# Three more batches of layer 1's keys and values made inside layer 0's quantized feed-forward, in a two-layer perceiver kernel

## The chip, the cores and the metric

The kernel runs on one core of one Trainium2 chip. The metric is the device time of one execution in microseconds (us); the median of three runs is compared. The core has four compute engines that each work through their own queue in order: PE (matrix multiply), DVE and ACT (elementwise work and reductions) and POOL (small work), and a fifth, SP, which here only issues DMA transfers.

## The reference, cut to what matters

Two layers work on `x` of 64 batches by 32 tokens by 256 features. Each has a cross-attention to a context of 257 rows a batch, a self-attention and a feed-forward, each on a layer norm of `x` and added to it. The change touches the feed-forward of layer 0 and the cross-attention of layer 1:

```python
def _L0_ffn_ref(x, w_gate, w_up, w_down):
    x = act_qdq(x)                                  # round to 16 bits, one scale for all of x
    up = act_qdq(x @ lpbq_dequant(w_up).T)
    gate = act_qdq(x @ lpbq_dequant(w_gate).T)
    sig = fixed_qdq_u16(jax.nn.sigmoid(gate))
    gate = act_qdq(gate * sig)
    o = act_qdq(gate * up)
    return o @ lpbq_dequant(w_down).T

def _L1_xattn_ref(x1, x2, Wq, bq, Wk, bk, Wv, bv, Wo, bo):
    q = x1 @ Wq.T + bq
    k = x2 @ Wk.T + bk                              # x2 is the context: 64 x 257 x 256
    v = x2 @ Wv.T + bv
    ...
    scores = jnp.einsum('bhnd,bhmd->bhnm', q, k) * scale
    attn = jax.nn.softmax(scores, axis=-1)
    o = jnp.einsum('bhnm,bhmd->bhnd', attn, v)
    ...
    return o @ Wo.T + bo

x = x + _L0_ffn_ref(_layernorm(x, axis=-1), ...)
x = x + _L1_xattn_ref(_layernorm(x, axis=-1), ctx_1024, ...)
```

`act_qdq` takes the largest absolute value of its whole input before it can round any of it, so the feed-forward is a row of stages with a global maximum between them. The keys and values of layer 1 depend on the context alone, not on `x`, so they can be made at any time.

## The kernel before, in words

**Keys and values made ahead.** Thirteen of layer 1's 64 batches (`AHEAD`, L566) have their keys and values made before layer 1 and kept in DRAM: four (`EARLY`) at the end of layer 0's self-attention, nine (`LATER`: 19, 23, ... 51) in its feed-forward. For one batch of `LATER`, `ahead_products` (L620) loads the batch's context, `ct`, over SP (two buffers), and issues 16 matmuls on PE: eight for the keys (`keys_of`, L591) and eight for the values (`values_of`, L602). Their results take three PSUM banks with the tag `mm`, of which there are six in this stage. `ahead_kept` is `ahead_keys` and `ahead_values`: on ACT two biased copies of the keys (L597, into `kb`, two buffers) and one copy of the values (L636, into `vb`, three buffers), and on SP two stores to DRAM, `dk` (L632) and `dv` (L638). The document calls an `ahead_kept` a keep.

**The stage between the up and the down projection.** The gate `g` and the up projection `u` each lie in 12 chunks of 128 x 1024. When the scale of the gate product is known, a loop over the chunks runs (L1147 on): `round_h(c + 1)` rounds a chunk of `g` and `round_up(n_up)` a chunk of `u`, both on ACT (L1108, L1105). `product(c)` multiplies the two on DVE and takes the maximum of the result (L1112 and L360); it needs `round_h(c)` and `round_up(c)` done. At some values of `c` the loop calls `keep_next` (L1139), which keeps the next batch and then issues the products of the batch after the next; so two batches' products are in flight, in the six banks. Two keeps and the first products stand before the loop (L1115 on, in the order written there), one keep behind it and two in the down projection. Behind the loop `scale_of` makes the scale of the output (`so`, `ro`), and `round_out` and `unbias` round it in blocks of 256 tokens, alternately on ACT and DVE. The down projection (L1185) takes a block at a time: 24 matmuls each.

**Layer 1's cross-attention** is a loop over the 64 batches, `f` (L1664 on), with the self-attention of the same layer interleaved in it, in steps that repeat every eight `f`. Step `f` issues `scores(f)` on PE, `weigh(f - 2)` on PE, `maxima(f)` on DVE (L1309), then the keys and values of batch `f + 1` (PE L591, L602; ACT L597; DVE L618), the exponentials `exps(f)` on ACT (L1316), `weights(f - 1)` on DVE (L1326, L1328) and the transposes `turn(f - 1)` on PE (L1347), whose results ACT and DVE copy. `scores(f + 1)` writes the same four PSUM banks that `exps(f)` reads. Where batch `f + 1` was made ahead, the step is "short" and in another order: its keys and values are loaded from DRAM (`kb` at step `f - 1`, L1700, `vb` in the step, L1716), no context is prefetched, and `weights(f - 1)` comes before `maxima(f)`, `turn(f - 1)` directly after it.

The order of the instructions on PE, DVE, ACT and POOL is the order of the program text there (`manual_schedule`). SP's order is left to the framework. Line numbers are those of the profile.

## Time and profile before

| | us |
|---|---|
| median of 3 runs (lowest, highest) | 1313.03 (1312.58, 1313.61) |
| the profiled execution, its own time | 1315.9 |
| its span, first to last instruction | 1314.0 |
| PE busy | 1221.6 (93%) |
| DVE busy | 908.0 (69%) |
| ACT busy | 722.1 (55%) |
| POOL busy | 157.9 (12%) |
| mean granted PE clock, of full | 0.977 |

A profile's page gives one execution. A group of instructions is named by its line, its engine, its operation and its tiles, as `out<-in`; `PEld` is the loading of weights into PE, which overlaps the matmuls. The chain of waits is followed back from the last instruction, at each step to what released it. In the timeline a row has the start, the time from there to the end of the last instruction of the row, the engine, the line, the operation and the number of instructions merged; in brackets stands the engine's idle time before it and what ended it. In a table of windows each row is a stretch of the span with its length, the busy time of each engine in it (and its number of instructions), and then the granted PE clock as a share of full speed, the share of time that the DMA engines were busy and what they moved in GB/s. All times are counted from the start of the span.

### The profile page before, as it was taken

The page shows a single profiled execution, that of the slowest core. Times are in us where ns is not written, and L with a number is a line of the kernel's source. Part 1 is how long each engine was busy: PE and PEld are TensorE (multiplying, and loading weights), DVE is VectorE, ACT ScalarE, POOL GpSimd, SP SyncE. Part 2 cuts the span into 40 slices and gives each one's busy share as a digit, 9 for nine tenths or more (in the row PEclk, how much of TensorE's full clock was granted, in tenths as well). Part 3 has the DMA queues.
Part 4 walks back from the last instruction along what each step waited for, and adds up shares of the span by engine and source line. Part 5 has one row for each costly group of instructions (what it writes and reads, how often), then busy time and mean ns, then how long its engine had stood idle before and what let it go on. Part 6 is the DMA issues. An engine that isn't in the chain of part 4 may idle for free.

```text
span 1314.0 us, 28426 instructions
## 1 busy us (share of the span) xinstructions
PE 1221.6 (93%) x11696; PEld 949.5 (72%) x11696; DVE 908.0 (69%) x1783; ACT 722.1 (55%) x1519; POOL 157.9 (12%) x418
## 2 busy tenths in 40 slices
PE   7899999999779998999999999998779999999998
PEld 5687877643568776767777777776557888888887
DVE  6878888768983688768788887868666363453633
ACT  4887887428792355657676766665525221221311
POOL 3111221000001022221212121211100000000000
PEclk9999999999999999989999999999769999999999
DMA  9200000630240442211111111100025000000000
GB/s 280 28 26 2 27 1 13 202 128 0 75 134 9 131 126 70 58 39 53 54 46 47 46 46 54 47 22 18 1 71 201 21 17 0 16 1 1 16 0 18
DMA packets 65430, 70.50 MB, mean 54 GB/s; under 512 B 21328, under 2 KB 52880, under 8 KB 65296
## 3 DMA queue, kind: packets, MB, share of 16 engines
q1 hardware_dynamic: 64864, 68.40, 17.7%
q8 instruction: 94, 1.54, 0.5%
q14 instruction: 40, 0.33, 0.1%
q10 hardware_dynamic: 432, 0.24, 0.1%
HBM read 59.63 MB, written 8.99 MB: 52 GB/s over the span
## 4 chain that ended last, share of the span: by engine, by line
PE 49%; DVE 15%; ACT 9%; issue 2%; DMA 2%; SPq 0%; POOL 0%; DVEq 0%; ACTq 0%
PE mm L1852 21%; PE mm L591 4%; PE mm L602 3%; PE mm L1347 3%; PE o L1185 3%; DVE nm L1309 2%; PE mm L397 2%; PE o L1919 2%; PE s L1298 2%; DVE mx L360 2%; DVE pe L1328 2%; ACT pe L1316 2%; ACT pb L312 2%; PE mm L348 1%; PE o L1367 1%
## 5 line engine op out<-in xcount | busy, mean ns | idle before, releaser
L1852 PE MATMUL mm<-hl,f_h 128*128 128x512 f32 x1024 | 232.9, 389 | 1.3 <-ACT sl L1897 1.3
L1852 PEld LDWEIGHTS mm<-hl,f_h 128*128 128x128 f32 x1024 | 192.1, 188 | 41.4 <-issue 1.5
L591 PE MATMUL mm<-ct,x_wk 128*128 128x257 f32 x512 | 132.5, 402 | 15.8 <-ACT kb L597 13.7
L1316 ACT ACTIVATE pe<-s,nm 128x257 f32<-128x257 f32 x256 | 118.5, 483 | 47.3 <-DVE nm L1309 20.8
L1910 ACT ACTIVATE g<-mm,cols 128x512 f32<-128x512 f32 x64 | 44.1, 689 | 163.9 <-PE mm L1852 163.5
L1858 DVE CAST hl<-g 128x512 fp32r<-128x512 f32 x64 | 27.3, 427 | 147.5 <-ACT g L1910 147.5
L591 PEld LDWEIGHTS mm<-ct,x_wk 128*128 128x128 f32 x512 | 95.6, 196 | 37.7 <-ACT kb L597 15.7
L602 PE MATMUL mm<-x_wv,ct 128*128 128x256 f32 x512 | 121.3, 380 | 0.3 <-ACT vb L636 0.3
L602 PEld LDWEIGHTS mm<-x_wv,ct 128*128 128x128 f32 x512 | 97.2, 190 | 14.4 <-ACT vb L636 0.7
L312 ACT ACTIVATE pb<-pt,masks 128x1024 f32<-128x1024 f32 x90 | 96.8, 1141 | 14.9 <-DVE pt L303 14.4
L597 ACT ACTIVATE kb<-mm,cols 128x257 f32<-128x257 f32 x128 | 57.8, 476 | 55.2 <-PE mm L591 51.3
L1309 DVE TENSOR_REDUCE nm<-s 128x4 f32<-128x1028 f32 x64 | 78.2, 1221 | 11.5 <-PE s L1298 11.5
L1336 POOL TENSOR_TENSOR px<-pe,rec 32x4 f32<-32x4 f32 x256 | 51.0, 199 | 264.7 <-DVE rec L1326 219.5
L1328 DVE TENSOR_SCALAR pe<-pe,rec 128x256 f32<-128x256 f32 x256 | 78.8, 370 | 5.7 <-DVE rec L1326 0.5
L1347 PE MATMUL mm<-ident,pe 128*128 128x128 f32 x512 | 75.9, 282 | 7.0 <-DVE pe L1328 4.5
L1347 PEld LDWEIGHTS mm<-ident,pe 128*128 128x128 f32 x512 | 59.2, 141 | 23.6 <-issue 5.9
L415 POOL TENSOR_TENSOR x<-x,rows 128x512 f32<-128x512 f32 x32 | 46.7, 1458 | 135.8 <-DVE xn L369 129.9
L1316 ACT ACTIVATION_READ_ACCUMULATOR pe<-s,nm 128x1 f32 x256 | 54.8, 214 | 0.0
L1298 PE MATMUL s<-kb,qb 32*64 32x257 f32 x1024 | 45.4, 409 | 8.9 <-ACT pe L1316 5.4
L1352 DVE COPY pT<-mm 128x512 f32<-128x512 f32 x64 | 44.0, 688 | 11.1 <-PE mm L1347 10.5
L1367 PEld LDWEIGHTS o<-pT,vb 128*32 128x32 f32 x2048 | 32.6, 112 | 25.1 <-issue 20.3
L618 DVE COPY vb<-mm 128x512 f32<-128x512 f32 x51 | 34.9, 685 | 21.2 <-PE mm L602 18.7
(238 smaller groups left out, 2363.4 us busy)
## 6 DMA issues: line engine op xcount, KB each, us to landing
ct<-in_ctxT_dram SPq DMA_DIRECT2D x64, 257.0 KB, 2.8
raw<-in_f_h_dram SPq DMA_DIRECT2D x20, 512.0 KB, 4.3
wck<-in_f_h_dram SPq DMA_DIRECT2D x12, 512.0 KB, 3.5
raw<-in_f_w_dram SPq DMA_DIRECT2D x8, 512.0 KB, 3.7
dk<-kb SPq DMA_DIRECT2D x13, 257.0 KB, 3.5
kb<-dk SPq DMA_DIRECT2D x13, 257.0 KB, 2.6
dv<-vb SPq DMA_DIRECT2D x13, 256.0 KB, 3.4
vb<-dv SPq DMA_DIRECT2D x13, 256.0 KB, 2.6
```

The costliest lines, as they stand in the source:

```text
L312: nc.scalar.activation(dst, src, AF.Copy, scale=scale)
L415: nc.gpsimd.tensor_tensor(xs, xs, bc(row(name), 1, 2), ALU.add)
L591: nc.tensor.matmul(pm, lhsT=x1_wk[:, k, m * P : (m + 1) * P], rhs=ct[:, k, :], start=(k == 0), stop=(k == 1),)
L597: nc.scalar.activation(kb[:, m, :], pm, AF.Identity, bias=col("x1_bk", m))
L602: nc.tensor.matmul(pm[:, c * D : (c + 1) * D], lhsT=ct[:, k, c * P : (c + 1) * P], rhs=x1_wv[:, k, :], start=(k == 0), stop=(k == 1),)
L1298: nc.tensor.matmul(sc[64 * m : 64 * m + 64, r, :S], lhsT=qb[rs, m, b % 4].rearrange("p h l -> p (h l)"), rhs=kb[rs, m, :], start=True, sto ...
L1309: nc.vector.tensor_reduce(w["nm"], w["sc"][:, :, :S], AX.X, ALU.max, negate=True)
L1316: nc.scalar.activation(w["pe"][:, r, :], w["sc"][:, r, :S], AF.Exp, bias=w["nm"][:, r : r + 1], accum_out=w["sums"][:, r : r + 1],)
L1328: nc.vector.tensor_scalar(pe[:, r, :SK], pe[:, r, :SK], rec[:, r : r + 1], None, ALU.mult)
L1336: nc.gpsimd.tensor_tensor(x4[j * L : (j + 1) * L, q // 2, :, q % 2], pe[of, :, SK], rec[of], ALU.mult)
L1347: nc.tensor.transpose(pt[:, r * P : (r + 1) * P], pe[:, r, c * P : (c + 1) * P], ident)
L1852: nc.tensor.matmul(pm, lhsT=w[:, k, c0 : c0 + P], rhs=hl[k][:, part, :], start=(k == 0 and part == 0), stop=(k == kt - 1 and part == 1),)
```

## The change

Batches 11, 25 and 41 are put in front of `LATER`, so 16 batches are made ahead instead of 13, and 48 are made in layer 1. In the loop between the up and the down projection `keep_next` is called at seven values of `c` instead of four, and `round_up` is called in every turn as long as chunks are left, also in those with a keep (so its last call is at `c` = 7 instead of 10). Behind the loop the program text is the same: one keep there and one in each of the first two blocks of the down projection. In layer 1, `f` = 10, 24 and 40 take the short order.

```diff
-    LATER, EARLY = tuple(range(19, 52, 4)), (15, 55, 59, 63)
+    LATER, EARLY = (11, 25, 41) + tuple(range(19, 52, 4)), (15, 55, 59, 63)
     AHEAD = LATER + EARLY
...
                 if c + 1 < NC:
                     round_h(c + 1)
                 product(c)
-                if c in (1, 4, 7, 11):
+                if c in (1, 3, 5, 7, 8, 10, 11):
                     keep_next()
-                elif n_up < NC:
+                if n_up < NC:
                     round_up(n_up)
                     n_up += 1
```

## The prediction, made before the changed kernel ran

> **What bounds the kernel now.** I read the page's chain of waits first: it runs mostly over PE (49%), then DVE (15%) and ACT (9%). Then I cut the span into the stages that the change touches: the rounding loop with the kept batches up to the first down-projection matmul (354.2 to 388.0), the down projection (388.0 to 437.2) and layer 1's cross-attention (437.2 to 911.7).

> ```profile
> core 0: us, PE busy (x) PEld busy (x) DVE busy (x) ACT busy (x) POOL busy (x), PEclk, DMA share, GB/s
> 354.20:388.00 33.80, 21.79 (x83) 17.39 (x83) 31.37 (x33) 30.99 (x37) 0.35 (x1) 0.90 0.36 117
> 388.00:437.20 49.20, 48.46 (x225) 41.63 (x224) 14.82 (x24) 14.86 (x18) 5.88 (x8) 1.00 0.17 50
> 437.20:911.72 474.52, 453.75 (x5678) 346.54 (x5682) 380.60 (x892) 312.66 (x923) 92.76 (x310) 0.99 0.20 57
> ```

> In the first stage PE idles for 12.0 us while DVE and ACT are full; in the other two PE is busy 98% and 96%. So products moved from the third stage into the first look free. Where the 12 us lie decides it, so next I read PE's timeline of the first stage.

> ```profile
> 366.14 2.00 PE L591 MATMUL mm<-ct,x_wk 128*128 128x257 f32 x8 [1.63 <-ACT kb L597]
> 367.98 1.89 PE L602 MATMUL mm<-x_wv,ct 128*128 128x256 f32 x8
> 373.00 3.46 PE L591 MATMUL mm<-ct,x_wk 128*128 128x257 f32 x8 [3.13 <-ACT kb L597]
> 376.30 1.89 PE L602 MATMUL mm<-x_wv,ct 128*128 128x256 f32 x8
> 380.99 2.00 PE L591 MATMUL mm<-ct,x_wk 128*128 128x257 f32 x8 [2.80 <-ACT kb L597]
> 382.84 1.89 PE L602 MATMUL mm<-x_wv,ct 128*128 128x256 f32 x8
> 384.56 1.90 PE L591 MATMUL mm<-ct,x_wk 128*128 128x257 f32 x8
> 386.30 1.89 PE L602 MATMUL mm<-x_wv,ct 128*128 128x256 f32 x8
> 388.03 2.32 PE L1185 MATMUL o<-wdnT,u 128*128 128x256 f32 x10
> ```

> Each idle stretch ends with ACT's biased keys: a product takes three of the six mm banks, so product n+2 waits until keep n (two biases and a copy on ACT) has emptied them. The last two products run without a gap into the down projection: its start at 388.03 is already set by PE. Back to back a product costs 384.56 − 380.99 = 3.57, then 388.03 − 384.56 = 3.47 us.

> **The change, part 1: the rounding loop.** Nothing is removed here. Three products (24 matmuls of L591, 24 of L602), six biases and three copies on ACT, three loads of ct and six stores (dk, dv) on SP's queue are added; POOL gets nothing. ACT's pitch comes from its timeline:

> ```profile
> 357.63 1.23 ACT L1108 ACTIVATE g<-g,magic,r 128x1024 f32<-128x1024 f32 x1
> 358.76 0.82 ACT L597 ACTIVATE kb<-mm,cols 128x257 f32<-128x257 f32 x2
> 359.48 0.57 ACT L636 COPY vb<-mm 128x512 f32<-128x512 f32 x1
> 359.95 1.25 ACT L1108 ACTIVATE g<-g,magic,r 128x1024 f32<-128x1024 f32 x1
> ```

> Start to start, a rounding costs 1.13 and a keep 359.95 − 358.76 = 1.19. From round_h(0) at 354.23 the new order puts ACT's keeps 2 to 8 at 358.8, 364.5, 370.2, 375.9, 379.4, 382.9 and 384.0, and keep 9 (the one behind the loop) at 385.2. Before, keeps 2 to 5 began at 358.8, 365.6, 372.5 and 380.5.

> DVE's product and maximum take 2.39 a chunk (355.50 to 357.89). Its last needs round_h(11), which starts at 381.7 instead of 376.8 (five keeps ahead instead of three, one more round_up). The small waits (chunk 5 0.6, chunk 7 0.9, chunk 9 1.0 us) move the last product from 381.76 to 384.3, and so ro from 385.76 to 388.3. Alone that would cost 2.6 us; the PE work behind it covers it.

> PE: keep 5 at 375.9 frees product 7, which starts 0.5 later (as 381.0 after 380.46), at 376.4. Products 7 to 11 then stand in line: 3.57 + 4 × 3.47 = 17.45, so the down projection starts at 393.9 instead of 388.03: **+5.8**. ACT's last keeps don't hold it up: keep 9 needs the store of keep 7 landed (kb has two buffers; dk stores there take 3.3 to 4.7 us) and ends by 388.3 to 389.6, before product 11 wants its banks at 390.4. ct 11 is asked for at 386.9 and lands 2.8 later, 0.7 before its use. Behind a late ct stand only PE's products and the whole down projection; behind a late store only ACT's round_out(1), which has 5 us of cover. The SP order isn't written out by hand: should a ct stand behind a store there, 1 to 2 us more. The down projection is dense on PE, so the delay reaches layer 1 whole.

> The granted clock adds to it:

> ```profile
> 355.52:358.94 3.42, 0.00 (x0) 0.00 (x0) 3.39 (x3) 3.42 (x4) 0.00 (x0) 1.00 0.29 77
> 358.94:362.35 3.41, 3.08 (x7) 2.52 (x8) 3.34 (x4) 3.41 (x6) 0.00 (x0) 0.50 0.41 154
> 369.18:372.59 3.41, 0.69 (x4) 0.26 (x2) 3.38 (x4) 3.41 (x5) 0.00 (x0) 1.00 0.29 77
> 372.59:376.00 3.41, 3.00 (x7) 2.45 (x8) 3.34 (x4) 3.41 (x6) 0.00 (x0) 0.50 0.40 154
> 560.32:563.74 3.42, 1.71 (x29) 1.17 (x18) 3.40 (x8) 2.11 (x8) 0.40 (x2) 1.00 0.25 77
> 563.74:570.56 6.82, 6.35 (x58) 4.60 (x59) 2.46 (x6) 2.88 (x9) 0.79 (x4) 0.50 0.01 2
> ```

> Here a stretch of 3.41 us with PE busy half or less is followed by one at 0.50, where eight key matmuls take 3.5 instead of 2.0. In the new loop PE idles some 2.1 us before product 6 and before product 7. If the second idle stretch falls mostly into one such window, product 7 is 1.5 late and so is all behind it; I give that two chances in five, +0.6. With 0.2 for a late ct the loop costs **+6.6**; bounds 2.6 (ACT and DVE alone) to 9.5 (5.8 + 1.7 clock + 2 SP).

> [...] The rows show two bursts cold and the one at 366.14 warm.

> **Part 2: layer 1, batches 11, 25 and 41.** Each leaves 16 matmuls, two biases, a copy on DVE and one ct load on SP, and gains two loads (kb, vb; 2.6 us each, issued one or two batches ahead, so hidden; ct's prefetch depth stays). Steps f = 10, 24, 40 become "short": weights(f−1) before maxima(f) on DVE, and turn(f−1) on PE without keys and values to cover its wait. PE's 3.5 us are therefore not the price; I lay the step out again with the offsets of the short step at 622 to 627 (turn 0.92 after the reciprocal, first exponential 2.65, last 4.6).

> ```profile
> 501.88:510.88 9.00, 9.00 (x89) 7.32 (x88) 7.79 (x16) 4.09 (x12) 0.79 (x4) 1.00 0.21 56
> 606.44:614.50 8.06, 7.96 (x82) 6.25 (x82) 7.48 (x27) 4.90 (x14) 2.30 (x7) 1.00 0.14 35
> 614.50:623.57 9.07, 8.91 (x86) 6.48 (x84) 6.19 (x17) 6.93 (x19) 1.55 (x8) 1.00 0.28 74
> ```

> f = 24: DVE is as full as PE (7.48 of 8.06), and loses only the copy (pitch 0.6 to 0.7). Reciprocal at 606.45, turn 607.4 to 608.7 (PE has idled 1.2), exponentials 609.1 to 611.0, queries until 610.5, scores(25) at 611.1 instead of 612.78. maxima(25) starts at 613.8 instead of 614.50, held by DVE. ACT, freed of two biases, reaches exps(25) at 615.3 instead of 617.09, turn(24) follows at 616.2 instead of 617.85, scores(26) at 620.3 instead of 621.96: **−1.6**. From there the old order holds and carries the shift. f = 40 has the same lengths (729.32 to 737.38 is 8.06): **−1.6**.

> f = 10: DVE sets it. Weights before maxima, no copy and no waits for it, and maxima(11) starts at 509.2 instead of 510.88: −1.7. But PE idles 1.3 us before turn(9) and 2.0 us before scores(11), with 1.75 us of work between; nearly every 3.41 us window there is half idle, as 560.32 was. Then scores, keys and values of f = 11 run partly at half clock, 1.4 us later, and turn(10), at 513.17 before, gains only 0.3. I take **−0.5**.

> That is −3.7; bounds −10.6 (PE's 3 × 3.53, if it alone set the pace) and −2.5. A loss is left out, since DVE, ACT and PE all have less to do in these steps.

> The same page's section "Why this matters for your kernels" asks only for no PE gaps over some 3 us. By that, f = 10 would lose nothing and part 2 would give −4.9; the 560.32 row, with a gap of 2.2, was followed by half clock.

> **Sum.** 1315.9 of the profiled execution + 6.6 − 3.7 = 1318.8 there (its span 1314.0 would become 1316.9). It stands 2.9 above the median of the runs, 1313.03; so I forecast **1315.9** for the median. A measurement of this kernel tells about 0.2%, 2.6 us, from no change: 1310.4 to 1315.65.

> **The rivals.**
> 1. *PE's whole price comes back.* Three batches at 3.53 save 10.6 against 6.6: 1309.0. For: PE is busy 96% in that stage. Against: DVE at 7.48 of 8.06 in f = 24 and the uncovered turn.
> 2. *The loop hides the products.* Only ACT's and DVE's 2.6 are paid, against 3.7: 1311.9. For: 12.0 us of idle PE. Against: 6.1 of it (4.45 and 1.63) lies before keep 3's product at 366.14, and five products need 17.45 us after 376.4.
> 3. *The crowd at the end becomes a new wait* (the other side): keeps 7, 8 and 9 come within 2.4 us where two came before, and stores, ct 10 and ct 11 share SP's queue. It decides when ct 11 lands after 390.4 or keep 9 ends after it. Loop 9.5, layer 1 −2.5 (clock): +7, 1320.0. For: dk landed in 4.7 us when two keeps met at 381. Against: PE's own line is long enough to hide 0.7.

> **How the numbers follow.** Forecast 0.55 (own range 1313 to 1318: 0.21 of it below 1315.65, 0.34 above), rival 1 0.12, rival 2 0.13 (0.12 same, 0.01 faster), rival 3 0.20. Faster 0.13, same 0.33, slower 0.54. The range runs from 1311.5, rival 2's time less 0.4, to 1321.0, rival 3's and 1.0 more; rival 1 and a tail above are left out.

> **What would show it.** Right: products 7 to 11 without gaps and the first L1185 matmul at about 394; ro near 388; scores(1) 6 to 7 later; f = 24 and f = 40 some 1.6 shorter over two steps; a stretch at 0.50 near f = 11. Wrong: L1185 before 391 (rival 2), or batch 25's two steps shorter by 3 (rival 1), or PE waiting for ct or ACT between products 9 and 11 (rival 3).

## The result, and the profile after

The changed kernel takes 1316.37 us (median of 14 runs, 1314.91 to 1320.0) against 1313.14 (14 runs, 1310.6 to 1318.02) before, a ratio of 1.0025 [1.0016, 1.0034]: 3.2 us slower. The prediction was 1315.9, some 2.9 slower.

The profiled executions differ by less, 1317.27 against 1315.9 (spans 1315.3 and 1314.0). The one of before had 23.9 us in a row at half clock at the end of layer 1's self-attention and 6.8 us of it near `f` = 19, and neither place is touched by the change; so they are compared stage by stage here, and the runs' medians are taken for the whole.

The windows of the three stages, after (the stretch with its length; busy us of each engine; granted clock; DMA share; GB/s):

```profile
core 0: us, PE busy (x) PEld busy (x) DVE busy (x) ACT busy (x) POOL busy (x), PEclk, DMA share, GB/s
355.32:397.97 42.65, 33.09 (x132) 26.51 (x131) 33.34 (x34) 37.63 (x50) 0.35 (x1) 0.92 0.50 152
397.97:447.15 49.18, 48.44 (x225) 41.62 (x223) 13.22 (x22) 11.93 (x14) 5.88 (x8) 1.00 0.16 48
447.15:914.66 467.51, 442.64 (x5618) 337.27 (x5622) 379.11 (x889) 310.11 (x917) 92.58 (x310) 0.99 0.21 59
```

The loop has grown from 33.80 to 42.65 us (42.62 from `round_h(0)`, as it is measured below), the down projection is the same (49.20, 49.18), and layer 1's cross-attention has shrunk from 474.52 to 467.51. PE's work moved as written (11.3 us more busy in the first stage, 11.1 less in the third, with some half clock in both figures). But 8.8 us were paid in the loop, where 12.0 us of PE lay idle. Of the 7.0 won in layer 1, only 4.0 belong to the three batches: over `f` = 19 and 20 before lost 3.0 to the half clock at 563.74, and after has full speed there.

The end of the loop on PE, after (start, us to the end of the row's last instruction, engine, line, operation, number; in brackets the idle time before it and what ended it):

```profile
377.58 3.61 PE L591 MATMUL mm<-ct,x_wk 128*128 128x257 f32 x8 [1.99 <-ACT kb L597]
380.98 2.02 PE L602 MATMUL mm<-x_wv,ct 128*128 128x256 f32 x8
382.83 1.90 PE L591 MATMUL mm<-ct,x_wk 128*128 128x257 f32 x8
384.57 1.89 PE L602 MATMUL mm<-x_wv,ct 128*128 128x256 f32 x8
386.73 1.97 PE L591 MATMUL mm<-ct,x_wk 128*128 128x257 f32 x8 [0.27 <-DMA ct<-in_ctxT_dram]
388.54 1.89 PE L602 MATMUL mm<-x_wv,ct 128*128 128x256 f32 x8
390.26 1.90 PE L591 MATMUL mm<-ct,x_wk 128*128 128x257 f32 x8
392.00 1.89 PE L602 MATMUL mm<-x_wv,ct 128*128 128x256 f32 x8
394.43 1.97 PE L591 MATMUL mm<-ct,x_wk 128*128 128x257 f32 x8 [0.54 <-DMA ct<-in_ctxT_dram]
396.24 1.89 PE L602 MATMUL mm<-x_wv,ct 128*128 128x256 f32 x8
397.97 1.24 PE L1185 MATMUL o<-wdnT,u 128*128 128x256 f32 x5
```

These are products 7 to 11. All times of after are 1.13 later here, because the stage begins that much later, ahead of any edit (`round_h(0)` at 355.35 instead of 354.23). Less that, product 7 starts at 376.45. Then PE works in line to the down projection. From there to 397.97 it takes 20.39 instead of 17.45. Three things make it longer: product 7's keys at half clock (3.61 instead of 2.00), and two waits for `ct`, before products 9 and 11. Counted from start to start the half clock is 1.7 of the 2.9, and the two waits, with the slower start behind each, 1.3 (their idle time alone is 0.8). A product that starts at full clock is called warm in what follows, one at half clock cold.

ACT's side of the same stretch, after:

```profile
383.96 0.86 ACT L597 ACTIVATE kb<-mm,cols 128x257 f32<-128x257 f32 x2
384.67 0.62 ACT L636 COPY vb<-mm 128x512 f32<-128x512 f32 x1
388.27 0.84 ACT L597 ACTIVATE kb<-mm,cols 128x257 f32<-128x257 f32 x2 [2.99 <-DMA dk<-kb]
391.59 0.84 ACT L597 ACTIVATE kb<-mm,cols 128x257 f32<-128x257 f32 x2 [2.00 <-DMA dk<-kb]
...
392.79 3.25 ACT L1167 ACTIVATE u<-u,magic,r 128x1536 f32<-128x1536 f32 x2
```

Keeps 8 and 9 wait 2.99 and 2.00 us for the stores of keeps 6 and 7, and ACT's `round_out(1)` behind them starts at 392.79. PE's line hides it: the down projection can't begin before 397.97 anyway, and then no wait for `u` stands before it. Why the stores are late is read from SP's queue, after (each row is the issue of one transfer):

```profile
383.02 0.38 SPq L580 DMA_DIRECT2D ct<-in_ctxT_dram  x1
383.50 0.42 SPq L632 DMA_DIRECT2D dk<-kb  x1
...
386.49 0.38 SPq L580 DMA_DIRECT2D ct<-in_ctxT_dram  x1
386.96 0.42 SPq L632 DMA_DIRECT2D dk<-kb  x1
...
390.46 0.38 SPq L580 DMA_DIRECT2D ct<-in_ctxT_dram  x1
```

A `ct` load can go only when the product two before it has ended and its buffer is free: 383.02 is the end of product 7, 386.49 of product 8, 390.46 of product 9. The keys of keep 6 were ready at 381.35 (its biases ran from 380.50 for 0.85), but its `dk` stood behind the load of 383.02 and went at 383.50; that of keep 7, ready at 384.82, stood behind the load of 386.49 and went at 386.96. The `dk` of keep 6 landed at 388.2, 4.7 us after its issue, and that is what keep 8 waited for. The last load, for product 11, was asked for at 390.46 and landed at 394.3, 3.8 us later; the prediction took 2.8. Over the whole execution a `dk` takes 4.0 us in the median, 3.5 before.

Layer 1: the windows of steps 24 and 25, after, cut at `maxima` as before:

```profile
core 0: us, PE busy (x) PEld busy (x) DVE busy (x) ACT busy (x) POOL busy (x), PEclk, DMA share, GB/s
614.03:619.99 5.96, 5.29 (x69) 3.97 (x70) 5.55 (x21) 5.23 (x14) 1.51 (x3) 1.00 0.09 33
619.99:628.16 8.17, 7.97 (x82) 5.68 (x80) 6.09 (x17) 5.80 (x18) 1.54 (x8) 1.00 0.27 83
```

The two steps took 17.13 and take 14.13, but 3.0 is not the gain: `maxima(24)` itself starts 1.3 later, because `weights(23)` now stands before it. Counted from `f` = 20 to 39, the shift against before goes from 6.26 to 4.56: 1.7 a batch. DVE is busy 5.55 of the 5.96 us, PE 5.29. For `f` = 10 the clock matters, so the next windows are those in which it fell, in the loop (first pair) and in steps 10 and 11 (second pair), after:

```profile
core 0: us, PE busy (x) PEld busy (x) DVE busy (x) ACT busy (x) POOL busy (x), PEclk, DMA share, GB/s
374.40:377.81 3.41, 1.42 (x7) 0.94 (x6) 2.84 (x3) 3.41 (x6) 0.00 (x0) 1.00 0.29 75
377.81:381.23 3.42, 3.42 (x9) 2.69 (x9) 2.53 (x3) 3.42 (x7) 0.00 (x0) 0.50 0.44 159
514.39:517.80 3.41, 1.35 (x49) 0.87 (x50) 3.38 (x6) 2.87 (x9) 0.00 (x0) 0.99 0.02 5
517.80:521.21 3.41, 3.41 (x9) 2.68 (x10) 3.38 (x9) 0.90 (x3) 0.38 (x1) 0.51 0.00 0
```

Each time a stretch of 3.41 us in which PE is busy 1.42 or 1.35 is followed by one at half clock in which PE is full. In the second pair the keys of batch 12 take 3.69 us, and `turn(10)`, at 513.17 before, comes at 522.91: 0.2 earlier than the 9.94 by which layer 1 begins later.

### The profile page after: what moved, and what is told of

Same layout as the page of the kernel before. It is cut to its first block, busy times and chain, and to the rows that moved or that the text cites. A ratio compares the mean times of both kernels' runs of the same rounds, so it can differ in the third digit from the quotient of the medians.

```text
span 1315.3 us, 28453 instructions
## 1 busy us (share of the span) xinstructions
PE 1222.7 (93%) x11696; PEld 950.8 (72%) x11696; DVE 907.0 (69%) x1780; ACT 722.5 (55%) x1522; POOL 157.6 (12%) x418
## 4 chain that ended last, share of the span: by engine, by line
PE 50%; DVE 16%; ACT 7%; issue 2%; DMA 1%; POOL 0%; DVEq 0%; ACTq 0%; POOLq 0%
PE mm L1852 21%; PE mm L591 5%; PE mm L602 4%; PE mm L1347 3%; PE o L1185 3%; DVE nm L1309 2%; DVE mx L360 2%; PE s L1298 2%; PE o L1919 2%; PE mm L397 2%; DVE pe L1328 2%; PE mm L348 1%; ACT pe L1316 1%; PE mm L1420 1%; PE o L1367 1%
## 5 line engine op out<-in xcount | busy, mean ns | idle before, releaser
L1852 PEld LDWEIGHTS mm<-hl,f_h 128*128 128x128 f32 x1024 | 192.1, 188 | 41.3 <-issue 1.4
L591 PE MATMUL mm<-ct,x_wk 128*128 128x257 f32 x512 | 132.4, 402 | 13.0 <-ACT kb L597 10.4
L602 PE MATMUL mm<-x_wv,ct 128*128 128x256 f32 x512 | 121.3, 380 | 0.1
L591 PEld LDWEIGHTS mm<-ct,x_wk 128*128 128x128 f32 x512 | 95.2, 195 | 35.4 <-ACT kb L597 12.4
L602 PEld LDWEIGHTS mm<-x_wv,ct 128*128 128x128 f32 x512 | 97.5, 191 | 14.4 <-ACT vb L636 0.5
L597 ACT ACTIVATE kb<-mm,cols 128x257 f32<-128x257 f32 x128 | 57.7, 477 | 54.5 <-PE mm L591 45.6
L385 ACT COPY xT<-mm 128x512 f32<-128x512 f32 x33 | 19.4, 589 | 55.3 <-PE mm L381 55.2
```

What stands on the lines that cost most here:

```text
L591: nc.tensor.matmul(pm, lhsT=x1_wk[:, k, m * P : (m + 1) * P], rhs=ct[:, k, :], start=(k == 0), stop=(k == 1),)
L597: nc.scalar.activation(kb[:, m, :], pm, AF.Identity, bias=col("x1_bk", m))
L602: nc.tensor.matmul(pm[:, c * D : (c + 1) * D], lhsT=ct[:, k, c * P : (c + 1) * P], rhs=x1_wv[:, k, :], start=(k == 0), stop=(k == 1),)
L1852: nc.tensor.matmul(pm, lhsT=w[:, k, c0 : c0 + P], rhs=hl[k][:, part, :], start=(k == 0 and part == 0), stop=(k == kt - 1 and part == 1),)
```

## The experiments

Twelve kernels, each compared with the kernel before on the same chip. The lengths of the stages come from each kernel's profile: the loop is from `round_h(0)` to the first down-projection matmul, steps 8 to 13 are cut at `maxima` (batch 11 is in them), and "rest" is from `maxima(63)` to the end, where no kernel has an edit.

| kernel | loop | steps 8–13 | 24, 25 | 40, 41 | rest | median (runs) | ratio to before [95%] |
|---|---|---|---|---|---|---|---|
| before | 33.80 | 42.66 | 17.13 | 18.19 | 402.30 | 1313.14 (14) | |
| after | 42.62 | 41.97 | 14.14 | 15.20 | 400.66 | 1316.37 (14) | 1.0025 [1.0016, 1.0034] |
| loop_only | 41.23 | 42.70 | 17.14 | 18.19 | 394.71 | 1319.46 (9) | 1.0039 [1.0026, 1.0053] |
| layer1_only | 33.83 | 42.79 | 14.14 | 15.20 | 399.51 | 1312.61 (12) | 0.9986 [0.9972, 0.9999] |
| round_up_only | 34.97 | 41.85 | 17.13 | 18.19 | 400.02 | 1314.03 (12) | 1.0 [0.9989, 1.0011] |
| two_batches | 36.58 | 42.89 | 14.14 | 15.20 | 398.57 | 1313.35 (12) | 0.9993 [0.9978, 1.0008] |
| early_keep | 38.38 | 42.66 | 14.13 | 15.18 | 401.78 | 1315.19 (12) | 1.0003 [0.999, 1.0017] |
| early_two | 37.66 | 42.41 | 14.14 | 15.18 | 399.40 | 1313.85 (12) | 0.9993 [0.9978, 1.0008] |
| own_ct | 39.80 | 41.73 | 14.14 | 15.19 | 401.24 | 1315.84 (12) | 1.0016 [1.0001, 1.0031] |
| warm | 41.87 | 41.95 | 14.14 | 15.19 | 399.88 | 1316.34 (12) | 1.0021 [1.0006, 1.0035] |
| best_two | 36.17 | 42.14 | 14.13 | 15.18 | 398.61 | 1312.23 (12) | 0.9992 [0.998, 1.0005] |
| best_three | 36.20 | 42.71 | 14.14 | 15.19 | 399.13 | 1312.04 (12) | 0.9987 [0.9972, 1.0002] |
| warm_step10 | 41.38 | 40.60 | 14.13 | 15.19 | 401.28 | 1316.93 (12) | 1.0021 [1.0005, 1.0038] |
| best_all | 36.19 | 40.86 | 14.14 | 15.20 | 400.97 | 1310.55 (12) | 0.9984 [0.9967, 1.0] |

The kernel before stood at 1314.33 beside loop_only to two_batches, at 1314.2 beside early_keep to warm, at 1313.43 beside best_two to warm_step10 and at 1313.27 beside best_all. The runs of one kernel spread over some 10 us, and a stage that no kernel touches varies by 7.6 between profiles. So a ratio of 12 runs is good to about 2 us either way, and an edit of 1 to 2 us is read from the stage that it is in.

One of these columns scatters by as much as is looked for in it. Steps 8 to 13 took 41.85 to 42.89 us in the six kernels in which layer 1 makes batch 11 itself and no step of them differs (before, loop_only, round_up_only, two_batches, early_two, best_two). The difference lies in step 12, where ACT waits for `px` of POOL, 0.98 us in round_up_only, 1.79 in before and 2.01 in two_batches; why it varies is open. In the six kernels that take batch 11 from DRAM and have nothing else changed there, the steps took 41.73 to 42.79. So the 0.7 between before and after is no measure of what batch 11 gives.

**The two halves apart.** In loop_only the loop is that of after, and layer 1 treats batches 11, 25 and 41 as before:

```diff
+    USED = tuple(b for b in AHEAD if b not in (11, 25, 41))
-    not_ahead = [b for b in range(B) if b not in AHEAD]
+    not_ahead = [b for b in range(B) if b not in USED]
...
-                short = f + 1 in AHEAD
+                short = f + 1 in USED
...
-                if f + 2 in AHEAD:
+                if f + 2 in USED:
```

> The changed kernel, with batches 11, 25 and 41 made and stored in the feed-forward as there, while layer 1 makes them itself again, in the order of before. So only the price of the loop is left. My theory (PE's line of five products at the end of the loop): the first down-projection matmul 5.8 to 9.5 us later in the span than in the kernel before, counted from the first rounding of the loop, and the time 6.6 (5.8 to 9.5) over before. Rival 2 (the idle PE hides the products): about 2.6 over before. Rival 1 (layer 1 gives PE's whole price, 10.6, back): since the whole change measured +3.2, the loop alone would have to cost about 13.8.

Measured: 5.1 us slower (3.4 to 7.0), less than the 5.8 to 9.5 expected. The loop itself is in that range: it took 41.23 us, 7.4 more than before, with product 7 at full clock and the last product waiting. The last two products on PE, loop_only:

```profile
391.27 1.89 PE L603 MATMUL mm<-x_wv,ct 128*128 128x256 f32 x8
394.15 1.98 PE L592 MATMUL mm<-ct,x_wk 128*128 128x257 f32 x8 [0.99 <-DMA ct<-in_ctxT_dram]
395.96 1.89 PE L603 MATMUL mm<-x_wv,ct 128*128 128x256 f32 x8
```

The last load was issued at 389.73 and landed 4.3 us later, and the product began 4.4 after the issue. Steps 8 to 13, 24, 25, 40 and 41 of layer 1 are those of before to 0.04 us.

In layer1_only, made from the kernel before, layer 1 runs the short steps and the loop is untouched:

```diff
+    USED = AHEAD + (11, 25, 41)
+    FROM = {b: AHEAD.index(b if b in AHEAD else 19) for b in USED}
...
-                    nc.sync.dma_start(bs[f + 2]["kb"], ahead[AHEAD.index(f + 2)]["k"])
+                    nc.sync.dma_start(bs[f + 2]["kb"], ahead[FROM[f + 2]]["k"])
```

with `USED` in place of `AHEAD` as above, and the same edit for `vb`.

> The kernel before, with its nine batches in the feed-forward, while layer 1 takes batches 11, 25 and 41 from DRAM in the short order. The stored keys and values that these three read are those of batch 19, so the attention of batches 11, 25 and 41 is computed with the keys and values of another batch. Only the gain is left. My theory: 3.7 less than before (bounds 2.5 to 4.9), with 1.6 to 1.7 each at steps 24 and 40 and a stretch of half clock near step 11 that eats most of the 1.7 of step 10. Rival 1: 10.6 less. Rival 2 needs 3.7 too, and differs in the loop alone.

Measured: 1.8 us faster (0.1 to 3.7), less than the 3.7 expected, which is the end of the interval. Steps 24, 25 and 40, 41 are 2.99 shorter each, exactly as in after. Batch 11 gained nothing, since here a stretch with PE busy 1.68 of 3.41 was followed by two at half clock, layer1_only:

```profile
core 0: us, PE busy (x) PEld busy (x) DVE busy (x) ACT busy (x) POOL busy (x), PEclk, DMA share, GB/s
502.79:506.20 3.41, 1.68 (x10) 1.16 (x10) 3.41 (x9) 1.74 (x6) 0.65 (x4) 1.00 0.60 191
506.20:513.00 6.80, 5.96 (x57) 4.29 (x58) 5.80 (x12) 2.68 (x9) 0.38 (x1) 0.50 0.01 2
```

The halves, +5.1 and −1.8, add up to +3.3; the whole change measured +3.2. Each half is good to 1.8 only, so the sum is a weak proof by itself. The stages say the same: the loss is made in the loop, the gain in layer 1.

**The order of `round_up` alone.** From the kernel before, `elif n_up < NC:` becomes `if n_up < NC:` and all else stays.

> The kernel before with the other half of the loop's edit alone: a chunk of the up projection is rounded in every turn, also in those with a keep; four keeps at the old places, no batch added. The keep of the last turn stays where ACT has the same work ahead of it, so my theory expects no change: within 0.5 of before, the first down-projection matmul at the same place. A theory that the new order itself costs (rounding the up projection earlier holds back DVE's products) expects 1 to 3 more.

The time was as expected (1.0 [0.9989, 1.0011]), the stage was not: here the other theory was right. The roundings moved forward delay the last ones of `g`, `ro` comes 1.36 us later, and the down projection waits for DVE, round_up_only:

```profile
386.77 1.89 PE L602 MATMUL mm<-x_wv,ct 128*128 128x256 f32 x8
389.44 2.86 PE L1185 MATMUL o<-wdnT,u 128*128 128x256 f32 x12 [0.77 <-DVE u L1170]
```

The stage is 1.17 longer. Half of what I took for the price of the added keeps on ACT and DVE (2.6) comes from this order. In after it costs nothing, for there PE is late by more.

**One batch less.** In two_batches `LATER` begins with (25, 41) instead of (11, 25, 41); the loop keeps its seven calls, the products of one batch fewer are issued in it, and no keep stands behind it.

> The changed kernel without batch 11: two more batches than before, the same seven keeps in the loop, so no keep is left behind the loop. My theory: one product less in PE's line, so the loop costs 2.4 by the line (3.57 + 3 x 3.47 from 376.4 gives 390.4 against 388.0), with clock and context loads 2.4 to 4.5, and layer 1 gives back 3.3 for batches 25 and 41: between 0.9 under and 1.2 over before, so 2 to 4 under the changed kernel. Rival 2 (only ACT and DVE's 2.6 are paid in the loop, whatever the number of products): 0.7 under before, but then the changed kernel would be no slower than that. Rival 1: 7.1 - 3.2 = 3.9 under before.

Measured: 36.58, 6.0 less than after, and 0.9993 [0.9978, 1.0008]. One product is 3.47 of this; the rest is after's half clock (1.7) and `ct` waits (0.8), which are absent here. So in these two profiles batch 11 costs 6.0 in the loop, and what it returns in layer 1 is within the scatter of steps 8 to 13; were product 7 warm in both, it would cost some 4.3 (an estimate, 6.0 less 1.7).

**Moving the gate of PE's line.** If the line is what is paid, it has to begin earlier. Its gate, in this text, is the moment from which it can run without further waits for ACT: the end of the keep that frees product 7's banks. In after, keep 2 stands behind the first chunk, and each product waits for a keep two before it. In early_keep, made from after, keep 2 is done before the loop:

```diff
             ahead_products(3)
+            ahead_kept(2)
+            ahead_products(4)
...
-            n_kept, n_up = 2, 4
+            n_kept, n_up = 3, 4
```

> The changed kernel with keep 2 and product 4 moved ahead of round_h(0), where ACT stood idle for 2.36 us waiting for the scale of the gate product and PE for 4.45; all later keeps move one place up, so the last product is issued inside the loop. My theory (PE's line decides): from the first rounding to the first down-projection matmul 36.2 to 37.8 (42.6 in the changed kernel's profile, 33.8 before), so 4 to 5 less time than the changed kernel, about the time of before (1.5 less to 0.5 more). A theory that ACT's and DVE's longer row of work sets the loop (ro 34.1 after the first rounding, in the changed kernel) expects that the loop gets no shorter than by one keep, 1.2.

Measured: 38.38, 4.2 less than after and much more than the 1.2 of the other theory, though over the 36.2 to 37.8 expected; the kernel's time can't be told from that of before, 1.0003 [0.999, 1.0017]. Product 8 ran at half clock (keys 2.86 us, values 2.76), which cost about 1.7 and takes it out of the range.

early_two joins this with (25, 41) and calls `keep_next` at `c` in (1, 3, 5, 8, 10, 11).

> As the run before, with batches 25 and 41 alone and keeps at turns 1, 3, 5, 8, 10 and 11. My theory: PE's line and DVE's scale end together, 35.0 to 36.2 after the first rounding (1.2 to 2.4 over before), layer 1 gives back 3.3: 0.9 to 2.1 under before, the fastest of the kernels so far. If batch 11 is worth its place (0.7 in the changed kernel's profile), this one is no faster than the one with all three.

A miss: 37.66, 1.1 longer than two_batches, which keeps the old start. Leaving out the turn at `c` = 7 gave PE 4.26 us of idle time before product 8; keys and values then took 2.83 and 2.80, and `ct` was 0.74 late as well. One gap more cost what the early start had won.

**The late `ct`.** own_ct, from after, loads the last two contexts into a part of a tile that is free there, so that they need not wait for a buffer:

```diff
-        ct = ctx_of(kv_pool, AHEAD[i], 2)
+        if i < 10:
+            ct = ctx_of(kv_pool, AHEAD[i], 2)
+        else:
+            ct = f0_xT[:, i - 8, :, 0:S]
+            nc.sync.dma_start(ct, ctx_v[:, :, AHEAD[i], :])
```

> The changed kernel, with the contexts of the last two products (10 and 11) loaded into two unused parts of the feed-forward's input tile, so that these loads need not wait until products 8 and 9 have released a buffer. My theory, with the term that was too small (a late context held product 11 back by 0.5 to 1.2): PE's line has no wait for a load, the loop is 0.7 to 1.6 shorter than in the changed kernel, the time 0.5 to 1.6 less. If SP's order (stores ahead of loads) is the cause and not the buffers, the wait stays and nothing changes.

Measured: 39.80. The waits are gone, own_ct:

```profile
389.58 1.89 PE L602 MATMUL mm<-x_wv,f_xT 128*128 128x256 f32 x8
391.31 1.90 PE L591 MATMUL mm<-f_xT,x_wk 128*128 128x257 f32 x8
393.04 1.89 PE L602 MATMUL mm<-x_wv,f_xT 128*128 128x256 f32 x8
394.77 1.46 PE L1189 MATMUL o<-wdnT,u 128*128 128x256 f32 x6
```

Product 7 was warm here too, which is why the loop is 2.8 shorter than after's and not 0.7 to 1.6. So this is the bare line: before's 33.80 and 6.0. The prediction's line is 5.85. What loop_only, where product 7 was warm as well, has over it, 41.23 − 39.80 = 1.4, is the late `ct`. The kernel's time moved with it only within its interval (1.0016 [1.0001, 1.0031]).

**The clock in the loop.** warm, from after, gives PE four matmuls that nobody reads (four calls; the trace counts two instructions for each, so x8), behind the keeps of turns 3 and 5, in the idle time before products 6 and 7:

```diff
+            def warm():
+                po = bank("o")
+                for i in range(4):
+                    nc.tensor.matmul(po[:, :D], lhsT=x1_wk[:, 0, :P], rhs=x1_wv[:, 0, :],
+                                     start=True, stop=True)
...
                     keep_next()
+                    if c in (3, 5):
+                        warm()
```

> The changed kernel with four more matmuls, into a bank that nobody reads, behind products 5 and 6, where PE would idle for 2.0 us each time: no work of the result is changed. My theory: PE's clock isn't at half when product 7 starts, whatever the place of the windows; eight key matmuls of product 7 take 2.0 instead of 3.6, the loop 1.0 to 1.7 less than in the changed kernel's profile, and the time 0 to 1.7 less, 0.7 in the mean. If the half clock has another cause, nothing changes, or the added matmuls cost up to 0.5.

The fillers and product 7, warm:

```profile
373.99 1.89 PE L1142 MATMUL o<-x_wv,x_wk 128*128 128x256 f32 x8
376.15 2.00 PE L591 MATMUL mm<-ct,x_wk 128*128 128x257 f32 x8 [0.27 <-ACT kb L597]
377.99 1.89 PE L602 MATMUL mm<-x_wv,ct 128*128 128x256 f32 x8
```

Product 7's keys are back at 2.00 us, and the fillers fit into the wait for ACT. That the fillers did it is not shown by this run alone: loop_only, two_batches, own_ct and warm_step10 have the same loop up to product 7 and no fillers, and product 7 was warm in all four. All runs together say more. Eleven idle stretches of 2.0 us without fillers stand before products in the loops changed this way, and three of them were followed by half clock (product 7 in after, 8 in early_keep, 6 in early_two). Twelve such stretches have fillers, in warm and in the three kernels that follow, and none was.

The loop is 41.87, only 0.75 shorter than after's where 1.0 to 1.7 was expected, because the line that starts warm reaches the `ct` loads earlier and waits longer for them (0.28 and 1.45). The two troubles cover each other: a line that is late by the half clock waits less for `ct`, so curing one of the two gave back less than its price (0.75 us here, where the half clock cost 1.7).

**The cures together.** best_three is early_keep with own `ct` from product 10 and fillers at turns 1, 3 and 5; best_two is the same for (25, 41), with `keep_next` at (1, 3, 5, 7, 10, 11), own `ct` from product 9 and fillers at 1, 3, 5 and 7.

> The same with all three batches: keeps at turns 1, 3, 5, 7, 8, 10 and 11, matmuls against the half clock behind products 5, 6 and 7. My theory: PE's line and the scale end 36.0 to 36.5 after the first rounding, 2.2 to 2.7 over before; layer 1 gives back 3.4 to 4.1: 0.7 to 1.9 less time than before, 2.5 to 4.5 less than the changed kernel. If batch 11 gave back the 1.7 that its step alone promises, this would be the faster of the two.

> What the runs so far found, put together for batches 25 and 41: keep 2 ahead of round_h(0), keeps at turns 1, 3, 5, 7, 10 and 11, the last two contexts in the unused part of the input tile, and four matmuls into an unread bank behind products 5 to 8 against the half clock. My theory: PE's line ends 34.9 to 35.3 after the first rounding, with DVE's scale (34.8): 1.1 to 1.5 over before; layer 1 gives back 3.3, so 1.8 to 2.2 less time than before, the fastest here. If something other than PE's line and the scale held the loop in the earlier runs, it stays over 36.5.

best_three: 36.20, so the three batches cost 2.4 in the loop instead of 8.8. Its steps 8 to 13 gained nothing (42.71), with half clock from 509.2 to 516. best_two: 36.17, no shorter, a miss: with one product less PE has to wait for DVE, 1.01 us, since `ro` comes 34.10 after the loop's start (the expectation had the scale end the stage at 34.8), as in best_three. Keeps at turns 1, 3, 5 and 7 are common to the two, and early_two, without the one at 7, had 33.13. So at 36.2 ACT's and DVE's chain ends the stage in best_two and PE's line in best_three, and the third batch is free there.

warm_step10, from after, has the same fillers behind `close_turn` at `f` = 10, where PE waits before `scores(11)`.

> The changed kernel with four matmuls into an unread bank in step 10 of layer 1, where PE waits some 2 us for the exponentials before scores(11). My theory: the window there is no longer half idle, the half clock near step 11 goes away, keys of batch 12 take 2.0 instead of 3.7 us, and steps 8 to 13 together (41.97 in the changed kernel's profile, 42.66 before) are 0.8 to 1.4 shorter than in the changed kernel's; the time 0.5 to 1.4 less. If the half clock isn't what eats batch 11's gain, the steps stay as long.

The filler and the keys of batch 12, warm_step10:

```profile
512.09 1.99 PE L1728 MATMUL mm<-x_wv,x_wk 128*128 128x256 f32 x8
514.19 0.69 PE L1298 MATMUL s<-kb,qb 32*64 32x257 f32 x16
...
515.40 2.01 PE L591 MATMUL mm<-ct,x_wk 128*128 128x257 f32 x8
```

The keys take 2.01 instead of 3.69, and steps 8 to 13 are 40.60, 1.37 less than after and less than in any kernel without these fillers. Each of the six kernels that take batch 11 from DRAM without fillers here had a stretch at half clock in these steps (after from 517.80, layer1_only from 506.20, best_three from 509.2), none of the six that make batch 11 in layer 1 had one, and this one has none. So what batch 11 failed to return was the clock. The kernel's own time doesn't show it (1.0021 [1.0005, 1.0038]); 1.4 us is at the limit of 12 runs here.

best_all joins best_three and the fillers of step 10.

> All three batches, the loop as in the run best_three (36.2 from the first rounding to the first down-projection matmul in its profile), and the four unread matmuls of step 10. My theory: 36.2 again, steps 8 to 13 at 40.6 to 41.3 (best_three 42.7, before 42.7), so layer 1 gives back 3.3 and another 1.4 to 2.1 against 2.4 in the loop: 2.3 to 3.0 less than before, a ratio of 0.9978 to 0.9983. A theory that the half clock only moves to another place when it is kept away from here expects the ratio of best_three, 0.9987.

The window of the loop (columns as above), then its last rows on PE, best_all:

```profile
355.98:392.17 36.19, 34.38 (x156) 28.57 (x154) 31.50 (x33) 33.34 (x43) 0.35 (x1) 1.00 0.53 162
```

```profile
390.44 1.89 PE L602 MATMUL mm<-x_wv,f_xT 128*128 128x256 f32 x8
392.16 6.08 PE L1200 MATMUL o<-wdnT,u 128*128 128x256 f32 x27
```

The loop runs at clock 1.00, PE is busy 34.38 of 36.19 us (about 5 of it the three fillers), and the last product hands over without a gap. The kernel took 1310.55 against 1313.27 before, 0.9984 [0.9967, 1.0]: by the ratio 2.1 us faster, which is the lowest median of all. By its stages it should be some 2.7 faster: 2.39 lost in the loop, 3.3 won with batches 25 and 41, 1.8 in steps 8 to 13. The interval ends at 1.0, so that it beats the kernel before is likely and not certain, and by time alone the ratio of best_three, 0.9987, isn't excluded either.

The theory that the half clock moves has something for it: there is one stretch of it in step 10, which begins ahead of the fillers, best_all:

```profile
504.24:507.65 3.41, 2.13 (x53) 1.22 (x53) 3.18 (x8) 1.57 (x4) 0.79 (x4) 1.00 0.95 317
507.65:511.07 3.42, 3.42 (x12) 3.07 (x13) 3.11 (x6) 2.90 (x10) 0.00 (x0) 0.50 0.19 65
```

It fell on `turn(9)` and on the fillers themselves (2.88 us instead of 1.99), and the keys of batch 12 were warm again (2.01); steps 8 to 13 are 40.86, 0.26 more than in warm_step10.

## Why the prediction was right

Less the 1.13 by which the stage starts later:

- **The line of products, +5.8: right.** Product 7 was put at 376.4 and came at 376.45; without late loads and without half clock in the line (own_ct) the loop grew by 6.0.
- **ACT and DVE, 2.6 late and covered: right.** Keeps 4 to 7 came at 370.20, 375.91, 379.37 and 382.83 where 370.2, 375.9, 379.4 and 382.9 stood; `ro` was put at 388.3 and was ready at 388.3 (389.41 less 1.13). About half of it is the order of `round_up` (round_up_only).
- **The half clock, +0.6 as a mean: right that it could fall on product 7.** Where it fell it cost 1.7 (after); in loop_only, two_batches, own_ct and warm_step10 product 7 was warm. So one of five loops with the same start was hit, where two chances in five stood. The reading that it rests on, busy half or less and then half clock, is too simple, as the last section shows.
- **The late `ct`, +0.2: the mis-sized term.** Its idle time is 0.8 (after's two waits) to 1.7 (warm's); loop_only against own_ct gives 1.4. The step that failed is "ct 11 is asked for at 386.9 and lands 2.8 later, 0.7 before its use". The load took 3.8 (after) and 4.3 (loop_only), among stores that took up to 4.7 in after, through one queue. That product 9 would wait too (0.27 in after, its load took 3.6) was not foreseen at all. The 1 to 2 us for a `ct` that stands behind a store were the author's estimate; in after's rows the stores of keeps 6 and 7 stood behind a `ct` (issued 0.48 and 0.47 after it).
- **Keep 8 at 384.0 and keep 9 by 388.3 to 389.6: wrong, and harmless.** Keep 8 began at 387.1, keep 9 ended at 391.8. I had taken the landing time of stores (3.3 to 4.7) but not that the `dk` of keeps 6 and 7 each stand 2.1 us in SP's queue, ready, behind a `ct` load that waits for product 7 or 8; and keep 8 was given no wait for keep 6's store. PE's line covered it.
- **Batches 25 and 41, −1.6 each: right,** 1.7 each. As a sign of rival 1 I had named "batch 25's two steps shorter by 3". They are, and it is no sign of it: the cut at `maxima(24)` moves with the order of the instructions by 1.3. A step whose order changes can't be measured between its own marks.
- **Batch 11, −0.5: the reason right, the size not shown.** The −0.7 over steps 8 to 13 lies within the scatter of that stage (1.0 in kernels that don't change it). That half clock eats the gain is shown: with the clock held up the steps are 1.4 shorter (warm_step10).
- **The sum, +2.9: right, as near as it is by luck.** +3.2 was measured. By the stages the loop was taken too low (7.4 with product 7 warm, 8.8 with it cold, against 6.6). Layer 1 gave 4.0 in the profile against 3.7, but 1.8 (0.1 to 3.7) in the runs of layer1_only, whose batch 11 gave nothing. By the runs of the halves, 5.1 and 1.8, both terms were taken too high, by 1.5 and 1.9, and the two errors cancel; both forecasts lie within the intervals, though.

Of the rivals, the first falls (1.7 a batch, not 3.5) and the second too: the line was paid in full, since PE's idle time in the new loop lies ahead of product 7's start, but for 0.8. The third was half there. Its condition came true, keep 9 and `ct` 11 were both later than 390.4, but the keep stayed under PE's line and only the load cost something, 0.8 to 1.7 instead of its 2.9.

In after's rows idle times of PE of 1.99 us before product 7 and 2.18 before `scores(11)` were followed by half clock. Of after's products 4 to 7 the first and the last were cold (keys 3.50 and 3.61 us) and the two between warm (2.00 each).

What stays open: each kernel has one profile, so how often product 7 is cold was not counted, and the 1.13 us ahead of the edits were not traced (over the fourteen profiles `round_h(0)` starts at 353.91 to 357.58, so they are within the scatter).

## What to carry to other kernels

Idle time of an engine is room only from the moment at which the work can start. Five products behind a gate at 376.4 cost their full length, though 9.2 of the 12.0 us that PE idled in the kernel before lay ahead of it; what pays is to move the gate (one keep earlier, 4.2 us), not the work. And buffers for the loads should grow with the work, here from two to four (own_ct, 1.4 us): with two, a line of products back to back asks for each load only as its predecessor but one ends.

## What the runs showed of the hardware

```profile
369.69:373.10 3.41, 1.62 (x7) 1.44 (x8) 3.34 (x4) 3.41 (x6) 0.00 (x0) 1.00 0.45 131
373.10:376.52 3.42, 2.11 (x10) 1.51 (x8) 2.52 (x3) 3.42 (x4) 0.00 (x0) 1.00 0.36 111
```

With the traces of before and after laid on their grids (from 20 to 1295 us), the next stretch was at half clock after all 19 stretches at full clock with PE busy up to 1.71 us (8 in before, 11 in after), and after 1 of 693 with more (1.97, in after). With own_ct's 1.62 and best_all's 2.13 beside them, what decides is open.

Where the grid lies to the code differs between the profiles: its first boundary behind `round_h(0)` comes 1.29 us after it in before and 1.97 in after. Five loops have the same code up to product 7, and there after lost 1.7 us at half clock, loop_only, two_batches, own_ct and warm_step10 nothing. How much half clock can differ over a long stretch is seen in the last stage, which no kernel edits. Before:

```profile
911.72:1314.00 402.28, 373.30 (x2130) 307.07 (x2122) 194.81 (x399) 116.91 (x173) 8.03 (x18) 0.95 0.09 30
```

and loop_only:

```profile
918.48:1313.20 394.72, 366.44 (x2110) 303.33 (x2110) 194.70 (x399) 116.86 (x173) 8.03 (x18) 0.98 0.09 31
```

The same code took 402.28 us at a clock of 0.95 and 394.72 at 0.98 (the clock stands third from the end). With matmuls that nobody reads where PE waits anyway, the keys behind them ran at full clock: 2.00 us for product 7 in warm where after had 3.61 (PE still waited 0.27 for ACT before it), and 2.01 in step 11 in warm_step10 where after had 3.69. In best_all those of step 10 were at half clock themselves, 2.88 us instead of 1.99.

Where stores and loads crowd at the end of the loop, a `dk` store of 257 KB took 4.7 us from issue to landing in after (median over the whole execution 3.5 in before and 4.0 in after, though before has one of 4.7 there too), and a `ct` load 3.8 in after and 4.3 in loop_only (median over the whole execution of before 2.8).
